# A four-part kernel on one core: router timing, weight splits, transposes and staging pools merged into one change

## The chip, the core and the metric

The kernel runs on one core of a Trainium2 chip. The core has five engines that run side by side and wait for each other through semaphores: TensorE for matmuls (PE in the profile; PEld are its weight loads), VectorE (DVE), ScalarE (ACT), GpSimd (POOL) and SyncE (SP). DMAs are issued from queues of SP, ACT and POOL. The metric is the device time of one execution in microseconds (us); lower is better. The text gives the median of several executions, and the profile shows one of them.

## The reference

The input x has 32 sequences of 128 tokens with 512 features, 4096 tokens in all. Four layers follow, the second and fourth with a residual around the pair they close:

```python
x = x + L0_ffn(L0_cond(x, cond))
x = x + L1_ffn(L1_cond(x, tokens, cond))

# L0_cond: two of eight experts per token, and one shared expert
shared = silu(x @ sw1.T) * (x @ sw3.T) @ sw2.T
s      = sigmoid(x @ router_w.T + cond @ router_t_w.T)   # the second term: one bias per sequence and expert
top2 of s + router_bias; gates from s; routed = sum of gate * (gelu(x @ rw1) @ rw2)
out    = (shared + routed) / 3
# L0_ffn: one of eight experts per sequence, chosen by its last token
logits = gelu(h[:, -1] @ Wp1 + bp1) @ Wp2 + bp2 ; sel = argmax(softmax(logits))
out    = h + 0.3 * ((gelu(h @ W1[sel] + b1[sel]) @ W2[sel] + b2[sel]) @ Wo + bo)
# L1_cond: one of 16 experts per token, given by a hash of the token, 256 slots each
xk, xr = mixes of x and the token before it
r      = sigmoid(xr @ w_recept.T) ; out = r * (relu(xk @ w_key) ** 2 @ w_value)
# L1_ffn: a scan over the 32 sequences as steps
f = sigmoid(x_t @ wf.T + c @ uf.T + bf); i, g likewise with wi, ui and wc, uc (g: tanh)
c = f * c + i * g
out = tanh(x @ wo.T + c_final @ uo.T + bo)
```

All data are float32.

## The kernel before, in words

Matmuls are made of split numbers. `split` (L61) writes a rounded copy, the high part, with ACT (L63) and the remainder, the low part, with DVE (L64). `mm3` (L76) then issues three matmuls for each block of 128 (L81): high by high, high by low, low by high. So every weight and every activation passes ACT and DVE once before PE may use it. `mm` (L54) is a plain matmul. A tile framework places the tiles in pools, adds the waits, and keeps the program's order on each engine except where its planner moves work; `tc.issue_after(ins)` orders what follows behind `ins` on the engine that `ins` runs on, and `behind` (L71) does it for both halves of a split.

The stages follow each other with little overlap:

- **A, 0 to about 310 us: the shared expert of token groups 0 to 3** (a group has 512 tokens, NG = 8). `shared` (L215) goes through eight weight columns a group (`KF`), each with `up`, `down` and the hooks `mid` and `hook2`. The weights come in pieces (`fetch_sw`, `split_sw`: raw tile swr, split swu and swd) through the raw pool of six buffers (L158). Group 0 also carries the router. `fetch_r` (L375) loads one 128-feature block of another group of x, `router` (L380) splits it and does the matmuls for rt with the router weights rwa and rwb, and zt is the copy of rt out of PSUM (L394). `mid0` (L592) spreads the 32 blocks over 16 half-steps by `cut` (L589), and calls `seq_bias` (L359), which sums the 512 features of cond times router_t_w over partitions by a matmul with ones into ps_tb. `choose`, `slots` and `invert` make the lists of tokens per expert. At the very start `fetch_x` (L203) loads group 0 on SP, and three copies of bias rows into the DRAM tensor bias_d (L726) stand on SP too.
- **Routed experts, about 310 to 558 us**: 71 blocks of 128 gathered tokens (xg, ptx, xb; `r_up`, `turn_h`, `r_down`), stored to o_d.
- **Shared expert of groups 4 to 7, 558 to 836 us**, with kept weights (kept_u), while `combine` (L747) adds shared and routed results, stores hid_d, and `policy` (L770) picks each sequence's expert. `hook2` (L939) calls, in the last group, `split_w` (L878) for the first three expert weights of the next stage, at the columns c = KF - AHEAD to KF - 1 with AHEAD = 3. `split_w(i)` splits piece i and then has `fetch_w(i + 3)` (L859) gather the next raw piece (rawB, 1 MB) by an indirect DMA on POOL into a pool of three buffers (wg, L711).
- **B, 836 to 1457 us: the per-sequence expert of L0_ffn and the mixes of L1_cond.** The loop over b (L1183 on) takes the sequences in an order sorted by expert, so that a weight is split anew only where the expert changes, four times. Iteration b does `up` (pu, then ue by ACT), `bend` (transposes pt, Gelu hf, split hb), `down` (po, then ps by ACT), and for the sequence before it `turn_r` (L1069): four transposes of ps into pr, then four times ACT with the bias (L1079) and DVE (L1080), which write the two halves of rT. Two sequences make a pair c. `close` (L1086) does the Wo matmuls of a pair (pb), adds the residual (x1, dx, xk) and, until the change, calls `mix_r` (L1134) for the other mix. In the odd iterations `send_k` (L1148: transposes ptB of xk, rows, a store to xk_d) and `send_v` (L1158: matmuls pv, r, a store to v_d) send the pair before. PSUM for all transposes of this stage is a pool of two buffers (ps_tB, L976); pt, pr and ptB take turns in it.
- **D, 1457 to 1834 us: the hashed experts** (`fetch_rows` gathers rowsD from xk_d by an indirect DMA; ptD transposes them; `use_piece` and its splits wD).
- **F, 1834 to about 2500 us: the scan.** `weight` (L1373) loads a 512x512 matrix in parts through a staging pool and splits it. `get_y` (L1406) gathers a block's y and loads r; `gate_y` (L1423) multiplies them, transposes (ptF) and splits into z. `from_x` and `from_c` (L1445, L1452) are the matmuls with z and with c. Until the change the staging pool is called stage and lives only for uf, wc, wi and wf (L1527 to L1540). After the last matmul a tail of output work follows up to the end.

Of the kernel before, what the change touches and what calls it, by code (L numbers as in the profile page):

```python
# [48 lines left out]
def tile_kernel(ctx: ExitStack, tc: tile.TileContext, a: dict, out: bass.AP):  # L49
# [106 lines left out]
    with ExitStack() as sa:  # L156
# [6 lines left out]
        def fetch(src, name):  # L163
            t = raw_p.tile([P, D], F32, tag="raw", name=name)
            nc.sync.dma_start(out=t, in_=src)
            return t

# [35 lines left out]
        def fetch_x(g):  # L203
            if g < NG:
                x_raw[g] = [fetch(a["x"][g][:, k, :], f"xraw_{g}_{k}") for k in range(KD)]
# [68 lines left out]
        with ExitStack() as s0:  # L274
# [31 lines left out]
            fetch_sw(1)  # L306
            ps_acc = s0.enter_context(tc.tile_pool(name="ps_acc0", bufs=4, space=PSUM, **kw))
# [51 lines left out]
            def seq_bias():  # L359

                ps = ps_r.tile([P, NB, E0], F32, tag="r", name="ps_tb")
                for k in range(KD):
# [7 lines left out]
                    mm(ps, ones, pr, k == 0, k == KD - 1)  # L370
# [218 lines left out]
            def cut(m):  # L589
                return min(NR, KD + (NR - KD) * (m - 1) // 15) if m > 0 else 0  # L590

            def mid0(n, w):  # L592

                if n < KF:
                    m = 2 * n + w
                    for i in range(cut(m), cut(m + 1)):
                        router(i)
                    for i in range(cut(m + 1), cut(m + 2)):
                        fetch_r(i)
                    if n + w == 1:  # L600
                        seq_bias()
# [124 lines left out]
        for kind, i in BIAS.items():  # L726
            nc.sync.dma_start(out=bias_d[:, bass.ts(i, KD)], in_=a[kind][:, KD * D :])
# [147 lines left out]
        def bias_of(kind, b, o):  # L875
            return bcol[b][:, BIAS[kind] * KD + o : BIAS[kind] * KD + o + 1]
# [21 lines left out]
        with ExitStack() as s2:  # L898
# [40 lines left out]
            def hook2(g, c):  # L939
                sums(g, c)  # L940
                if g == last:
# [22 lines left out]
    with ExitStack() as sb:  # L964
# [37 lines left out]
        def seq(p):  # L1002

            if p not in seqs:
                seqs[p] = nc.sync.value_load(seq_i[0:1, p : p + 1], min_val=0, max_val=PARTS[where(p)[0]] - 1)
            return seqs[p]

        def rows_of(t, p):

            return t[bass.ds((seq(p) + where(p)[0] * PARTS[0]) * P, P), :]  # L1010
# [58 lines left out]
        def turn_r(b):  # L1069
# [7 lines left out]
            for o in range(KD):  # L1077
                hi = rTs[c][:, 0, o, bass.ts(j, P)]
                done_a = nc.scalar.activation(hi, pt[:, o, :], AF.Identity, bias=bias_of("W2a", b, o))  # L1079
                done_v = nc.vector.scalar_tensor_tensor(  # L1080
                    rTs[c][:, 1, o, bass.ts(j, P)], pt[:, o, :], bias_of("W2a", b, o),
                    hi.bitcast(F32), ALU.add, ALU.subtract,
                )
            return done_a.ins, done_v.ins
# [63 lines left out]
        def send_k(b):  # L1148
# [5 lines left out]
            done = nc.scalar.copy(rows, pt.rearrange("p k q -> p (k q)"))  # L1154
            nc.sync.dma_start(out=rows_of(xk_d, b), in_=rows)
            return done.ins
# [21 lines left out]
        for b in range(-1, NB + 1):  # L1178
            c, j = divmod(b - 1, PB)
            if b + 1 < NB:  # L1180
# [28 lines left out]

            pair = b - 3 if b % 2 and 0 <= b - 3 < NB - 2 else None  # L1210
# [15 lines left out]
            if pair is not None and pair < NB - 6:  # L1226
                send_v(pair)
            if b + 1 < NB:
                bend(b + 1, "b")
            if pair is not None and pair < NB - 6:  # L1230
                send_v(pair + 1)
            if j == PB - 1 and 0 <= c < NB // PB:
                wo_done, k_done = close(c, b == NB)
                fetch_xh(c + 1)
                if c < NB // PB - 2:
                    mix_r(c, bp, "xr")
                elif c == NB // PB - 2:
                    mix_r(c, end_p, "xr")
# [3 lines left out]
        for b in range(NB - 2, NB):  # L1242
            rows_done = send_k(b)
# [11 lines left out]
    with ExitStack() as sd:  # L1255
# [97 lines left out]
        for p in range(NPC):  # L1353
# [14 lines left out]
            if p == NPC - 9:  # L1368
# [4 lines left out]
                def weight(name, pool, stage, bufs, tag="raw", parts=2, queue=nc.sync):  # L1373

                    pair = pool.tile([P, 2, KD * D], FR, tag=name, name=f"{name}_hl")
# [14 lines left out]
    with sf:  # L1390
        kw = dict(reuse_waits="tile")
        ZS = 2
        uf_p = sf.enter_context(tc.tile_pool(name="uf_p", bufs=1, side="right", **kw))
# [12 lines left out]
        def get_y(b):  # L1406

            y = yp.tile([P, D], F32, tag="y", name=f"y_{b}")
            nc.gpsimd.indirect_dma_start(  # L1409
# [5 lines left out]
            ys[b] = (y, r)  # L1415

        LEAD = 2
        for b in range(LEAD):
            get_y(b)
# [3 lines left out]
        def gate_y(b):  # L1423
# [11 lines left out]
            split(zs[g][:, 0, :, s], zs[g][:, 1, :, s], pt)  # L1435
# [9 lines left out]
        def from_x(t, ps, which, start, stop):  # L1445
            g, j = divmod(t, GB)
            for n in which:
                if start:
                    ps[n] = ps_g.tile([P, D], F32, tag="g", name=f"ps_{n}_{t}")
                mm3(ps[n], lambda h, k: zs[g][:, h, k, bass.ts(j, P)], lambda h, k: wx[n][:, h, k, :], KD, start, stop)  # L1450

        def from_c(t, n, ps, cT, start, stop):  # L1452
            if start:
                ps[n] = ps_g.tile([P, D], F32, tag="g", name=f"ps_{n}_{t}")
            mm3(ps[n], lambda h, k: cT[:, h, k, :], lambda h, k: uc[n][:, h, k, :], KD, start, stop)
# [16 lines left out]
        def unit(n, k0=0, k1=KD):  # L1472
# [15 lines left out]
            elif g >= NG - 1 - ZS:  # L1488
                zos[g, o] = zop.tile([P, GT], F32, name=f"zok_{g}_{o}")
# [237 lines left out]
```

## Time and profile before

| what | us |
|---|---|
| median of three runs | 2526.67 |
| the runs | 2529.47, 2526.67, 2520.85 |
| the profiled execution | 2522.89 |
| its span | 2521.2 |
| PE busy / idle in the span | 2455.6 / 65.6 |
| PE idle by stage: 0:310, 310:558, 558:836, 836:1457, 1457:1834, 1834:2500, 2500:2521 | 12.7, 2.2, 1.1, 19.5, 3.9, 5.0, 21.0 |
| DVE busy by the same stages | 237.5, 125.0, 177.1, 284.3, 262.4, 231.2, 14.1 |
| ACT busy by the same stages | 153.9, 97.3, 94.6, 316.4, 235.7, 158.1, 8.5 |
| mean granted TensorE clock of the span | 0.989 |

A busy share says how long an engine had an instruction in hand; the matmuls are pipelined, so a busy PE can still be slow, which the granted clock shows (1.00 is full speed). In the lists of waits a line names the engine and the instruction that stood still, what it stood for after the arrow, and then the time in all, how often, and the longest. In a list of stretches each engine's busy time stands before its number of instructions, and the granted clock, the DMA share and GB/s come last.

### The profile page before, as it was taken

The page shows a single profiled execution, that of the slowest core. Times are in us where ns is not written, and L with a number is a line of the kernel's source. Part 1 is how long each engine was busy: PE and PEld are TensorE (multiplying, and loading weights), DVE is VectorE, ACT ScalarE, POOL GpSimd, SP SyncE. Part 2 cuts the span into 40 slices and gives each one's busy share as a digit, 9 for nine tenths or more (in the row PEclk, how much of TensorE's full clock was granted, in tenths as well). Part 3 has the DMA queues.
Part 4 walks back from the last instruction along what each step waited for, and adds up shares of the span by engine and source line. Part 5 has one row for each costly group of instructions (what it writes and reads, how often), then busy time and mean ns, then how long its engine had stood idle before and what let it go on. Part 6 is the DMA issues. An engine that isn't in the chain of part 4 may idle for free. (4 is left out here: it accounts for less than half of the span.)

```text
span 2521.2 us, 37055 instructions
## 1 busy us (share of the span) xinstructions
PE 2455.6 (97%) x13044; PEld 2074.9 (82%) x13044; DVE 1331.5 (53%) x2341; ACT 1064.6 (42%) x1935; POOL 429.6 (17%) x460
## 2 busy tenths in 40 slices
PE   8999999999999899999999999999999999999996
PEld 5688899987888788888887889999978888888885
DVE  7797644556567444444454477667643323333336
ACT  4444533343223555455455466666532212222224
POOL 1000022222233333323223010000010000000003
PEclk9999999999999999999999999999999999999998
DMA  5545544457565333342342387776441111111027
GB/s 180 165 125 168 180 151 154 156 184 249 176 217 168 113 107 127 116 134 70 104 146 96 123 295 226 231 234 224 139 160 42 38 38 38 43 42 42 25 80 267
DMA packets 193117, 351.11 MB, mean 139 GB/s; under 512 B 37473, under 2 KB 72337, under 8 KB 189857
## 3 DMA queue, kind: packets, MB, share of 16 engines
q1 hardware_dynamic: 141504, 244.42, 29.6%
q0 software_dynamic: 36160, 74.90, 10.3%
q10 hardware_dynamic: 15264, 29.37, 3.2%
q8 instruction: 108, 1.77, 0.3%
q14 instruction: 81, 0.66, 0.1%
HBM read 373.94 MB, written 88.13 MB: 183 GB/s over the span
## 5 line engine op out<-in xcount | busy, mean ns | idle before, releaser
L64 DVE TENSOR_TENSOR wD<-rawD,wD 128x1024 fp32r<-128x1024 f32 x128 | 156.4, 1229 | 77.4 <-ACT wD L63 77.2
L81 PE MATMUL p<-xhl,swu 128*128 128x512 f32 x768 | 188.0, 396 | 5.5 <-ACT xhl L63 5.5
L81 PEld LDWEIGHTS phD<-xe,wD 128*128 128x128 f32 x1536 | 184.6, 189 | 1.2
L81 PE MATMUL phD<-xe,wD 128*128 128x256 f32 x1536 | 185.3, 281 | 0.0
L81 PE MATMUL p<-xhl,kept_u 128*128 128x512 f32 x768 | 184.3, 394 | 0.7 <-DVE kept_u L64 0.7
L81 PE MATMUL poD<-wD,hD 128*128 128x512 f32 x768 | 181.3, 392 | 0.0
L81 PEld LDWEIGHTS p<-xhl,swu 128*128 128x128 f32 x768 | 143.8, 189 | 36.0 <-ACT xhl L63 5.8
L81 PEld LDWEIGHTS p<-xhl,kept_u 128*128 128x128 f32 x768 | 141.8, 188 | 30.1 <-DVE kept_u L64 1.1
L81 PEld LDWEIGHTS poD<-wD,hD 128*128 128x128 f32 x768 | 142.0, 188 | 28.4
L63 ACT CAST wD<-rawD 128x1024 fp32r<-128x1024 f32 x128 | 133.1, 1046 | 53.4 <-PE poD L81 48.7
L278 POOL DMA_INDIRECT xg<-in_x_rows_dram,blk_t x71 | 67.6, 952 | 463.4 <-PE ptx L288 257.8
L1409 POOL DMA_INDIRECT y<-res_d,gat_i x32 | 33.3, 1040 | 573.9 <-DVE r L1428 495.2
L81 PE MATMUL pur<-r,xb 128*128 x852 | 118.2, 288 | 0.7 <-DVE xb L64 0.4
L81 PE MATMUL por<-r,hbr 128*128 x426 | 116.3, 407 | 1.4 <-ACT hbr L63 1.3
L64 DVE TENSOR_TENSOR xb<-ptx,xb 128x512 fp32r<-128x512 f32 x71 | 49.1, 692 | 115.3 <-ACT xb L63 115.3
L81 PEld LDWEIGHTS pur<-r,xb 128*128 128x128 f32 x852 | 105.2, 189 | 1.7 <-ACT xb L63 0.7
L81 PE MATMUL ps_f<-wf_hl,z 128*128 128x512 f32 x384 | 96.5, 399 | 0.0
L81 PE MATMUL poF<-z,wo_hl 128*128 128x512 f32 x384 | 96.4, 399 | 0.0
L81 PE MATMUL acc<-swd,as 128*128 128x512 f32 x384 | 96.0, 395 | 0.0
L81 PE MATMUL ps_c<-wc_hl,z 128*128 128x512 f32 x384 | 95.1, 395 | 0.7 <-ACT z L63 0.7
L81 PE MATMUL pb<-rT,Wo_hl 128*128 128x256 f32 x768 | 94.6, 281 | 0.0
L81 PE MATMUL pv<-w_recept_hl,xr 128*128 128x512 f32 x384 | 94.3, 395 | 0.0
(1014 smaller groups left out, 5038.3 us busy)
## 6 DMA issues: line engine op xcount, KB each, us to landing
rawD<-in_w_key_dram SPq DMA_DIRECT2D x64, 512.0 KB, 4.1
rawD<-in_w_value_dram SPq DMA_DIRECT2D x64, 512.0 KB, 3.8
swr<-in_sw_dram SPq DMA_DIRECT2D x120, 256.0 KB, 3.7
o_d<-obr SPq DMA_DIRECT2D x71, 256.0 KB, 2.4
xraw<-in_x_dram SPq DMA_DIRECT2D x32, 256.0 KB, 3.8
rraw<-in_rw_dram SPq DMA_DIRECT2D x32, 256.0 KB, 3.4
xc<-in_x_dram SPq DMA_DIRECT2D x32, 256.0 KB, 3.5
hid_d<-o ACTq DMA_DIRECT2D x32, 256.0 KB, 2.2
```

What stands on the lines that cost most here:

```text
L63: first = nc.scalar.copy(hi, src).ins
L64: done = nc.vector.tensor_tensor(lo, src, hi.bitcast(F32), ALU.subtract).ins
L81: done = nc.tensor.matmul(ps, lhsT=left(hl, k), rhs=right(hr, k), start=start and k + n == 0, stop=stop and 3 * k + n == last,)
L278: nc.gpsimd.indirect_dma_start(out=xg[i], out_offset=None, in_=a["x_rows"], in_offset=bass.IndirectOffsetOnAxis(ap=blk_t[:, i : i + 1], ax ...
L1409: nc.gpsimd.indirect_dma_start(out=y, out_offset=None, in_=res_d, in_offset=bass.IndirectOffsetOnAxis(ap=gat_i[:, b : b + 1], axis=0),)
```

## The change

It merges four edits to separate stages with some at the start:

- `fetch_x`: the pieces k = 0 and 2 of group 0 are issued by ACT, the others by SP.
- Router: `cut` starts at the fourth half-step instead of the second, router loads have six buffers of their own (xrr) and run two half-steps ahead. `seq_bias` adds the four products on DVE and uses one matmul group; it is called at the end of group 0.
- The bias rows are copied behind the last store of the routed experts.
- `split_w` for the first three pieces of stage B runs at c = 4, 5, 6.
- `turn_r`: one DVE add of the bias over the whole tile and one split. `mix_r` moves to the odd iteration after `close`; `send_v` moves to the even iterations, before `turn_r` and after `down`.
- The helpers `fetch`, `seq`, `rows_of`, `send_k`, `weight` and `bias_of` take a queue, a tile or a count as an argument; `get_y`, `gate_y`, `from_x` and `from_c` return their last instruction. `first_loads` is the last load of `fetch_sw(1)`.
- The last two `send_k` store from ACT's queue, with the row number read by ACT.
- Scan: one staging pool zop of four buffers for wc, uf, wi (SP) and wf (POOL), which later also holds the zok tiles; wo is staged after the second z, and the f matmuls of step 0 follow its c and i.

The diff without those helpers:

```diff
...
@@ -202,7 +204,10 @@
             if g < NG:
-                x_raw[g] = [fetch(a["x"][g][:, k, :], f"xraw_{g}_{k}") for k in range(KD)]
+                x_raw[g] = [
+                    fetch(a["x"][g][:, k, :], f"xraw_{g}_{k}", nc.scalar if g == 0 and k % 2 == 0 else nc.sync)
+                    for k in range(KD)
+                ]
...
@@ -358,7 +364,7 @@
-                ps = ps_r.tile([P, NB, E0], F32, tag="r", name="ps_tb")
+                sum_ = None
                 for k in range(KD):
@@ -367,7 +373,11 @@
                     )
-                    mm(ps, ones, pr, k == 0, k == KD - 1)
+                    if k > 0:
+                        nc.vector.tensor_tensor(pr, pr, sum_, ALU.add)
+                    sum_ = pr
+                ps = ps_r.tile([P, NB, E0], F32, tag="r", name="ps_tb")
+                mm(ps, ones, sum_, True, True)
                 nc.vector.tensor_copy(tbias, ps)
@@ -375,7 +385,9 @@
                 if 0 < g < NG:
-                    xrs[i] = fetch(a["x"][g][:, k, :], f"xr_{g}_{k}")
+                    xrs[i] = rt.tile([P, GT], F32, tag="xrr", bufs=6, name=f"xr_{g}_{k}")
+                    with tc.issue_after(first_loads):
+                        nc.sync.dma_start(out=xrs[i], in_=a["x"][g][:, k, :])
@@ -587,7 +599,7 @@
             def cut(m):
-                return min(NR, KD + (NR - KD) * (m - 1) // 15) if m > 0 else 0
+                return min(NR, KD + (NR - KD) * (m - 3) // 13) if m > 2 else 0
@@ -595,10 +607,8 @@
                         router(i)
-                    for i in range(cut(m + 1), cut(m + 2)):
+                    for i in range(cut(m + 2), cut(m + 3)):
                         fetch_r(i)
-                    if n + w == 1:
-                        seq_bias()
@@ -606,6 +616,8 @@
                     next(steps[0], None)
+                    if c == KF - 1:
+                        seq_bias()
                     return
@@ -723,8 +735,9 @@
-        for kind, i in BIAS.items():
-            nc.sync.dma_start(out=bias_d[:, bass.ts(i, KD)], in_=a[kind][:, KD * D :])
+        with tc.issue_after(stored):
+            for kind, i in BIAS.items():
+                nc.sync.dma_start(out=bias_d[:, bass.ts(i, KD)], in_=a[kind][:, KD * D :])
         os_, shs = {}, {}
...
@@ -943,9 +956,9 @@
                             fetch_w(n)
-                    if c >= KF - AHEAD:
+                    if 4 <= c < 4 + AHEAD:
                         with behind(act_split):
-                            split_w(c - KF + AHEAD)
+                            split_w(c - 4)
...
@@ -1074,14 +1089,13 @@
                 rTs[c] = rTp.tile([P, 2, KD, PB * P], FR, tag="rT", name=f"rT_{c}")
-            for o in range(KD):
-                hi = rTs[c][:, 0, o, bass.ts(j, P)]
-                done_a = nc.scalar.activation(hi, pt[:, o, :], AF.Identity, bias=bias_of("W2a", b, o))
-                done_v = nc.vector.scalar_tensor_tensor(
-                    rTs[c][:, 1, o, bass.ts(j, P)], pt[:, o, :], bias_of("W2a", b, o),
-                    hi.bitcast(F32), ALU.add, ALU.subtract,
-                )
-            return done_a.ins, done_v.ins
+
+            rT = ps.rearrange("p (k q) -> p k q", k=KD)
+            bias = bias_of("W2a", b, 0, KD).unsqueeze(2).to_broadcast([P, KD, P])
+            nc.vector.tensor_tensor(rT, pt, bias, ALU.add)
+            s = bass.ts(j, P)
+            split(rTs[c][:, 0, :, s], rTs[c][:, 1, :, s], rT)
+            return tuple(last_split)
...
@@ -1182,11 +1195,16 @@
                 fetch_hid(b + 3)
+            gated = b - 4 if b % 2 == 0 and 0 <= b - 4 < NB - 6 else None
+            if gated is not None:
+                send_v(gated)
             if 0 <= b - 1 < NB:
...
                 used()
+            if gated is not None:
+                send_v(gated + 1)
             if b == -1:
@@ -1206,6 +1224,10 @@
+
+            if j == 0 and 0 < c < NB // PB:
+                with behind(last_split) if b + 1 < NB else nullcontext():
+                    mix_r(c - 1, end_p if c == NB // PB - 1 else bp, "xr")
@@ -1223,24 +1245,16 @@
                 used()
-            if pair is not None and pair < NB - 6:
-                send_v(pair)
             if b + 1 < NB:
                 bend(b + 1, "b")
-            if pair is not None and pair < NB - 6:
-                send_v(pair + 1)
             if j == PB - 1 and 0 <= c < NB // PB:
...
                 fetch_xh(c + 1)
-                if c < NB // PB - 2:
-                    mix_r(c, bp, "xr")
-                elif c == NB // PB - 2:
-                    mix_r(c, end_p, "xr")
...
         for b in range(NB - 2, NB):
-            rows_done = send_k(b)
+            rows_done = send_k(b, nc.scalar)
         with tc.issue_after(k_done), tc.issue_after(rows_done):
...
@@ -1390,6 +1405,8 @@
+
+        zop = sf.enter_context(tc.tile_pool(name="zop", bufs=4, side="right", **kw))
         uf_p = sf.enter_context(tc.tile_pool(name="uf_p", bufs=1, side="right", **kw))
...
@@ -1486,7 +1505,9 @@
             elif g >= NG - 1 - ZS:
-                zos[g, o] = zop.tile([P, GT], F32, name=f"zok_{g}_{o}")
+                if o % 2 == 0:
+                    zok = zop.tile([P, 2, GT], F32, tag="raw", name=f"zok_{g}_{o}")
+                    zos[g, o], zos[g, o + 1] = zok[:, 0, :], zok[:, 1, :]
                 nc.scalar.copy(zos[g, o], po)
@@ -1524,21 +1545,23 @@
         ps, wx = {}, {}
-        with tc.tile_pool(name="stage", bufs=4, side="right", **kw) as stage:
-            uc["f"] = weight("uf", uf_p, stage, 4)
-            for b in range(LEAD):
-                nc.scalar.activation(ys[b][1], ys[b][1], AF.Sigmoid)
-            for n in "cif":
-                from_c(0, n, ps, cT, True, False)
-            wx["c"] = weight("wc", wx_p, stage, 4, queue=nc.scalar)
-            with tc.issue_after(first_part["wc"]):
-                gate_y(0)
-                gate_y(1)
-            for b in range(LEAD):
-                get_y(b + LEAD)
-            for n in "if":
-                wx[n] = weight("w" + n, wx_p, stage, 4, queue=nc.scalar)
-        zop = sf.enter_context(tc.tile_pool(name="zop", bufs=1, **kw))
+
+
+        wx_hl = {n: wx_p.tile([P, 2, KD * D], FR, tag="w" + n, name=f"w{n}_hl") for n in "ifc"}
+        wx["c"] = weight("wc", wx_p, zop, 4, pair=wx_hl["c"])
+        uc["f"] = weight("uf", uf_p, zop, 4)
+        wx["i"] = weight("wi", wx_p, zop, 4, pair=wx_hl["i"])
+        for b in range(LEAD):
+            nc.scalar.activation(ys[b][1], ys[b][1], AF.Sigmoid)
+        for n in "cif":
+            from_c(0, n, ps, cT, True, False)
+        gate_y(0)
+        z_done = gate_y(1)
+
+        with tc.issue_after(first_got):
+            wx["f"] = weight("wf", wx_p, zop, 4, pair=wx_hl["f"], queue=nc.gpsimd)
+        for b in range(LEAD):
+            get_y(b + LEAD)
         bias = {n: load_row("b" + n, D, keep_p) for n in "cif"}
@@ -1546,13 +1569,16 @@
             if t == 0:
-                from_x(0, ps, "cif", False, True)
-                wo1 = weight("wo", keep_p, yp, 2, "zo", KD)
+                done = from_x(0, ps, "ci", False, True)
+                with tc.issue_after(done):
+                    from_x(0, ps, "f", False, True)
+                with tc.issue_after(z_done):
+                    wo1 = weight("wo", keep_p, yp, 2, "zo", KD)
                 for n in "cif":
...
                 for n in "cif":
-                    from_c(t, n, ps, cT, False, True)
+                    late = from_c(t, n, ps, cT, False, True)
                     gate(t, n, ps, v, bias)
@@ -1589,8 +1615,9 @@
                     split(uo1[:, 0, k], uo1[:, 1, k], raw)
-                load_part(first_p, "c0", "x", 3, 0)
-                load_part(first_p, "cT0", "x", 3, 1, 2)
+                with tc.issue_after(late):
+                    load_part(first_p, "c0", "x", 3, 0)
+                    load_part(first_p, "cT0", "x", 3, 1, 2)
                 load_part(yp, "zo", "x", 3, 3)
...
             if t == NB - 2:
```

More of the change, by code (lines that the diff above doesn't have):

```diff
@@ L161, in tile_kernel, with fetch @@
         xgp = sxg.enter_context(tc.tile_pool(name="xgp", bufs=3, **kw))
-        def fetch(src, name):
+        def fetch(src, name, queue=nc.sync):
             t = raw_p.tile([P, D], F32, tag="raw", name=name)
-            nc.sync.dma_start(out=t, in_=src)
+            last_load[:] = [queue.dma_start(out=t, in_=src).ins]
             return t
+        last_load = []
         NSW = KF * NG
@@ L306, in tile_kernel @@
             fetch_sw(1)
+            first_loads = last_load[0]
             ps_acc = s0.enter_context(tc.tile_pool(name="ps_acc0", bufs=4, space=PSUM, **kw))
@@ L873, in fetch_w, with bias_of @@
                     )
-        def bias_of(kind, b, o):
-            return bcol[b][:, BIAS[kind] * KD + o : BIAS[kind] * KD + o + 1]
+        def bias_of(kind, b, o, n=1):
+            return bcol[b][:, BIAS[kind] * KD + o : BIAS[kind] * KD + o + n]
         def split_w(i):
@@ L1000, in tile_kernel, with seq, rows_of @@
         seqs, end_p = {}, None
[L1002 to L1010, printed above, removed]
+        def seq(p, queue=nc.sync):
+            if (p, queue) not in seqs:
+                seqs[p, queue] = queue.value_load(
+                    seq_i[0:1, p : p + 1], min_val=0, max_val=PARTS[where(p)[0]] - 1
+                )
+            return seqs[p, queue]
+        def rows_of(t, p, queue=nc.sync):
+            return t[bass.ds((seq(p, queue) + where(p)[0] * PARTS[0]) * P, P), :]
         xs = {}
@@ L1146, in mix_r, with send_k @@
             split(xrs[c][:, 0], xrs[c][:, 1], dx)
-        def send_k(b):
+        def send_k(b, queue=nc.sync):
             c, j = divmod(b, PB)
@@ L1153, in send_k @@
             rows = rp.tile([P, D], F32, tag="rows", bufs=2, name=f"rows_{b}")
-            done = nc.scalar.copy(rows, pt.rearrange("p k q -> p (k q)"))
-            nc.sync.dma_start(out=rows_of(xk_d, b), in_=rows)
-            return done.ins
+            nc.scalar.copy(rows, pt.rearrange("p k q -> p (k q)"))
+            return queue.dma_start(out=rows_of(xk_d, b, queue), in_=rows).ins
         def send_v(b):
@@ L1371, in tile_kernel, with weight @@
                 uc, first_part = {}, {}
-                def weight(name, pool, stage, bufs, tag="raw", parts=2, queue=nc.sync):
-                    pair = pool.tile([P, 2, KD * D], FR, tag=name, name=f"{name}_hl")
+                def weight(name, pool, stage, bufs, tag="raw", parts=2, queue=nc.sync, pair=None):
+                    if pair is None:
+                        pair = pool.tile([P, 2, KD * D], FR, tag=name, name=f"{name}_hl")
                     flat = a[name].rearrange("p k n -> p (k n)")
@@ L1408, in get_y @@
             y = yp.tile([P, D], F32, tag="y", name=f"y_{b}")
-            nc.gpsimd.indirect_dma_start(
+            got = nc.gpsimd.indirect_dma_start(
                 out=y, out_offset=None, in_=res_d,
@@ L1415, in get_y @@
             ys[b] = (y, r)
+            return got.ins
         LEAD = 2
         for b in range(LEAD):
-            get_y(b)
+            first_got = get_y(b)
         zp = sf.enter_context(tc.tile_pool(name="zp", bufs=2, **kw))
@@ L1434, in gate_y @@
             s = bass.ts(j, P)
-            split(zs[g][:, 0, :, s], zs[g][:, 1, :, s], pt)
+            return split(zs[g][:, 0, :, s], zs[g][:, 1, :, s], pt)
         def turn(c, t):
@@ L1449, in from_x @@
                     ps[n] = ps_g.tile([P, D], F32, tag="g", name=f"ps_{n}_{t}")
-                mm3(ps[n], lambda h, k: zs[g][:, h, k, bass.ts(j, P)], lambda h, k: wx[n][:, h, k, :], KD, start, stop)
+                done = mm3(ps[n], lambda h, k: zs[g][:, h, k, bass.ts(j, P)], lambda h, k: wx[n][:, h, k, :], KD, start, stop)
+            return done
         def from_c(t, n, ps, cT, start, stop):
@@ L1454, in from_c @@
                 ps[n] = ps_g.tile([P, D], F32, tag="g", name=f"ps_{n}_{t}")
-            mm3(ps[n], lambda h, k: cT[:, h, k, :], lambda h, k: uc[n][:, h, k, :], KD, start, stop)
+            return mm3(ps[n], lambda h, k: cT[:, h, k, :], lambda h, k: uc[n][:, h, k, :], KD, start, stop)
         def gate(t, n, ps, v, bias):
```

## The prediction

> **What bounds the kernel now.** I read the busy times first, then what the tensor engine (PE) waits for, then the clock around the longest waits, then single rows. The page's first line:
>
> ```profile
> PE 2455.6 (97%) x13044; PEld 2074.9 (82%) x13044; DVE 1331.5 (53%) x2341; ACT 1064.6 (42%) x1935; POOL 429.6 (17%) x460
> ```
>
> PE is the bound: of 2521.2 us it is idle for 65.6, of which 21.6 are the tail after the last matmul and 44 lie between matmuls. A matmul of 128x512 starts every 0.227 us (12 take 2.72), and the change touches almost none of them. So it can win holes, the slow clock behind holes, and few matmuls. The waits of PE (total us, times, longest) name the holes:
>
> ```profile
> PE pt_0a L1050 <- ACT ue_0a L1043: 7.0, 1, 7.0
> PE p L81 <- ACT xhl L63: 5.5, 1, 5.5
> PE ptD L1304 <- DMA rowsD<-xk_d,slot_t: 3.9, 3, 1.7
> PE rt L55 <- DVE rwa L356: 3.0, 1, 3.0
> PE ptF L1433 <- DVE z L64: 2.9, 1, 2.9
> PE pt_6a L1050 <- ACT o L756: 2.6, 1, 2.6
> PE ptB L1152 <- ACT hf_26a L1053: 2.5, 1, 2.5
> PE pt_15a L1050 <- DVEq L891: 2.1, 1, 2.1
> PE ptB L1152 <- ACT hf_16a L1053: 2.0, 1, 2.0
> PE ps_tb L55 <- ACT zt L394: 1.9, 1, 1.9
> ```
>
> Ten rows hold 33 of the 44 us, and all but the second lie in stages that the diff touches. Below them come nine waits of ptB for an hf of 0.2 to 0.5 us, 3 together. Stretches (PE, PEld, DVE, ACT, POOL busy, then the granted clock):
>
> ```profile
> 0.00:50.00 50.00, 39.61 (x155) 28.07 (x156) 32.40 (x77) 23.95 (x40) 8.95 (x28) 0.97 0.58 177
> 835.00:855.00 20.00, 13.04 (x52) 10.39 (x51) 7.12 (x11) 9.53 (x17) 7.21 (x7) 0.74 0.79 276
> 1834.00:1869.00 35.00, 30.65 (x129) 23.93 (x128) 20.20 (x26) 18.50 (x25) 10.43 (x9) 0.90 0.69 227
> ```
>
> A clock of 0.74 over 20 us is 5.2 us of clock missing. By the same product: 1.5 in 0 to 50, 1.8 at 930 to 950 (0.91), 1.6 at 1105 to 1145 (0.96), 1.5 at 1315 to 1330 (0.90), 3.4 at 1455 to 1470 (0.77), 3.5 at 1834 to 1869. Everywhere else in the middle it is full. So holes of about 2 us and more cost again behind them.
>
> **The skill.** "TensorE: Matmul & The Clock Gate", What's actually happening: half the clock after an idle window of about 3.4 us, full again after a busy one, with a window that runs on its own. The trace agrees in size (one piece is worth 1.5 to 1.8, half of 3.4) but not in the threshold: holes of 1.9 to 2.6 us brought it on too. "DMA: Bandwidth & Descriptors", Issuing engines are not separate DMA queues: another issuing engine saves only issue time. The trace agrees: the first weight and the x pieces land some 1.1 us apart per 256 KB, so part 1 is priced at nothing. "ScalarE: Activation LUTs", What ACT_TABLE_LOAD costs: 1.28 us for a load; the trace has 1.28 at 12.88, and part 7 meets one.
>
> **The change, part by part** (against the profiled execution of 2522.9 us; it is 3.8 below the median of 2526.7, inside the runs' spread of 8.6).
>
> 1. *Two of the first x pieces issued by ACT, bias rows away from the start.* First matmul still at 5.5: 0 (-0.5 to +1).
>
> 2. *Router from the fourth sub-step on with its own six buffers; one matmul group for the biases, at the end of group 0.* The first router matmul waits 3.0 us for rwa, which the DVE makes at 17.75 behind setup work; four matmuls later nothing waits. The bias sum's hole is 1.9. Its matmuls:
>
> ```profile
> L55 PE MATMUL ps_tb<-pr,ones x16: 379/380/696, 28.7 to 34.4; 128*128 128x256 f32 x16
> ```
>
> Eight of them pass in 2.49 us, about half of it at the slow clock, so 0.25 each at full clock; a quarter remains, 12 x 0.25 = 3.0 less. Clock 1.5. Two waits for zt near 67 and 97 (1.0 and 1.1) move with the router; I count half, 1.0. Added: three DVE adds of 0.42. Sum 3.0+1.9+3.0+1.5+1.0 = 10.4, with a little of the mode switching gone 11 (4 to 13). The cover is the DVE: it is 83.4 of the first 110 us busy, and the router's same work is pressed from 15 into 13 sub-steps. On SP the weight pieces stand behind router loads, each waiting for one of six buffers until its split.
>
> 3. *Bias rows sent after the routed store.* Three SP issues of about 0.6 us stand ahead of swr_34; that piece was split at 565 to 568 and wanted at about 572, so it had 2 to 5 us in hand: +0.5 (0 to +3).
>
> 4. *The first three weight splits of stage B one column earlier (c = 4, 5, 6).* The stall at that stage's start:
>
> ```profile
> 845.38 1.04 ACT L63 CAST wB_W2b<-rawB 128x1024 fp32r<-128x1024 f32 x1 [7.39 <-DMA rawB<-in_W2b_dram,idxw]
> ...
> 846.54 0.59 ACT L1043 COPY ue_0a<-pu_0a 128x512 f32<-128x512 f32 x1
> ...
> 847.18 1.11 PE L1050 MATMUL pt_0a<-ident,ue_0a 128*128 128x128 f32 x4 [6.96 <-ACT ue_0a L1043]
> ```
>
> ue_0a stands on ACT behind the cast of W2b, whose gather was issued at 835.7 and took 9.7. The gather waits for the buffer that the split of W2a frees; one column (about 8 us) earlier it is issued at 827.5 and lands at 837, before ue_0a is wanted at 840.2 (where the hole begins). The hole of 7.0 goes, and of the 5.2 of clock the part in which matmuls ran (842.3 to 852.6 at half, the hole until 847.2: 5.4/2 = 2.7). Sum 9.7; 9 taken (5 to 10.5).
>
> 5. *Stage B.* turn_r's four ACT activations (0.37) and four DVE operations (0.35), each waiting for the other, become one DVE add (128x512 from PSUM, 0.69 as such rows take), one cast (0.62) and one subtract (0.69). DVE work is the same (1.40 and 1.38), ACT falls by 0.86 a sequence. The old form's waits:
>
> ```profile
> L1080 DVE SCALAR_TENSOR_TENSOR rT<-pr,b,rT x128: 339/351/355, 867.7 to 1438.0; 128x128 fp32r<-128x128 f32 x128
> ...
>   ACT rT L1079: 56.8, 56
> ```
>
> mix_r leaves close for the following odd step, behind the weight split; send_v goes to even steps, so ptB's transposes directly follow those of pt_a and no longer wait for Gelu (hf) to free a PSUM buffer. Gone: the four holes at expert changes 2.6+2.1+2.0+2.5 = 9.2, of which ptB keeps 2.6 (in two of them it now waits 1.3 for the add); the small waits, 3; clock 3.5 of 4.9; one switch between transposes and matmuls a pair, 0.2 by the rows' spacing, 15 times, 3. That is 16 if no new wait comes; I take two thirds, 11 (2 to 14).
>
> 6. *The last two key rows on ACT's queue.* rows_31's store waits for rows_30's landing, as before, and ACT now stands behind it for 2.75 us; r_28 and the last mix cast follow. The gathers of stage D come about 1.7 earlier: of the holes 3.9 and the clock 3.4, 2 are won (4 won to 2 lost).
>
> 7. *Start of the scan.* One pool of four staging buffers, order wc, uf, wi on SP, wf on POOL, wo after the second z. Before, PE waited 0.7 and 2.9 and 0.6 here. Now ACT must cast wc, uf and wi, load a table and take the two sigmoids before the first z; wi's pieces wait for the DVE to split wc (1837 to 1838), r behind them on SP lands 4 to 6 us later (SP's row of before: 5.44 for two issues). So ptF stands at 1847 to 1848, PE's last ps_f ends at 1842.4: one hole of about 5 instead of 4.2 in three, with the same clock behind: +1 (-3 to +6).
>
> 8. The scan's steady part and the tail keep their order on every engine: 0.
>
> Sum: 0-11+0.5-9-11-2+1 = -31.5. From the profile 2491.4, from the median 2495.2; **2494**.
>
> **Rivals.** *Half is won (2510).* Group 0 becomes DVE-bound (85% where the router is pressed together) or the weights come late behind router loads, part 2 gives 2 instead of 11; or B's holes merely change their owner, part 5 gives 3 and the start of the scan costs 4: -31.5+9 or +11 = -22 to -20 for one, -12 for both. For it: the wait for rwa names a DVE that is behind, and clock windows are all or nothing. Against: 25% of the DVE is free there.
>
> *The stage-B pair is now tied to the DVE (slower, 2553).* ptB needs turn_r's PSUM buffer, which only one DVE add frees; where this add stands behind a weight split (1.23 each, two a piece) PE waits in all 16 pairs. From about 2 us a pair on the clock falls too, 1.7: 3.7 x 16 = 59 on 2494. It decides from 2.4 us a pair without clock loss (39/16), from about 2 with it. Against: DVE was busy 25.4 of 60 us in steady B (870 to 930), and the add is its first work after pr; only expert changes come near.
>
> *The edits cancel (2526).* Clock windows move rather than vanish, scan start at +6, bias rows +3, ACT behind its own store +2. Needs three ends at once.
>
> *It doesn't do what it says.* The order that the scheduler gives after the change shows the moves: router after three sub-steps, ptB behind pt_a, four bias instructions. Excluded.
>
> **How the numbers follow.** Chances: all or most won 0.62, half 0.25, nothing 0.06, slower by a pair's wait or by the scan's start 0.07. About 0.3% (7.6 us) is what a measurement of this kernel can tell from no change, so faster is 0.87. The main case's own range is 2483 to 2506. For 8 in 10 the half case comes in: 2480 (ends of parts 2, 4, 5 and 6 together, -43) to 2515.
>
> **What would show it.** The waits of rt for rwa, ps_tb for zt and pt_0a for ue_0a absent; PEclk 1.0 in 0 to 50 after the first microseconds and near the start of stage B; ps_tb four instructions; ptB's waits for hf gone, at most two for DVE rT of 1 to 2 us; ptD's wait under 2.5; one ptF hole near 5. PE busy about 2440. The forecast is wrong if p waits for weight pieces in group 0, if ptB waits for rT in most pairs, or if the ptF hole passes 8.

## The result and the profile after

The changed kernel takes 2504.98 us (median of four runs, 2502.66 to 2510.3) against 2524.09 for the kernel before (the three runs above and one more of 2521.5): a ratio of 0.9926, with a 95% interval from 0.9904 to 0.9947. It is faster by 19 us where 31.5 were forecast, and inside the stated range. The profiled execution of the changed kernel is its slowest of the four, 2510.3 with a span of 2508.6, so the two profiles differ by 12.6 and not by 19.

The first line of the page and the waits of PE after the change (total us, times, longest):

```profile
PE 2446.4 (98%) x13030; PEld 2071.8 (83%) x13030; DVE 1332.5 (53%) x2275; ACT 1038.9 (41%) x1839; POOL 414.1 (17%) x462
```

```profile
PE po L81 <- DVE hb_0a L64: 7.1, 1, 7.1
PE p L81 <- ACT xhl L63: 6.3, 1, 6.3
PE acc L81 <- ACT as L63: 6.0, 1, 6.0
PE acc L81 <- DVE as L64: 2.6, 1, 2.6
PE phD L81 <- DVE hf L1337: 2.3, 1, 2.3
PE ptF L1451 <- DVE r L1446: 2.2, 1, 2.2
PE rt L55 <- DVE rwa L362: 2.1, 1, 2.1
```

PE is still idle for 62.2 us of the span (2508.6 less 2446.4), where it was idle for 65.6. The waits of ptB for hf, of pt_0a and pt_15a and of ps_tb are gone, and pt_6a waits 0.6 where it waited 2.6. New are two long ones, acc for as (8.6 us in two pieces) and po for hb_0a (7.1), a wait of 2.3 of phD for hf, and a few of under 2 us that are not shown here.

The stretches around them (PE, PEld, DVE, ACT, POOL busy, then the granted clock, DMA share and GB/s):

```profile
0.00:50.00 50.00, 41.61 (x172) 30.25 (x173) 39.18 (x106) 27.63 (x46) 8.77 (x28) 1.00 0.68 223
550.00:580.00 30.00, 20.68 (x75) 15.72 (x74) 16.70 (x29) 11.62 (x21) 8.00 (x11) 0.83 0.76 227
845.00:865.00 20.00, 12.87 (x51) 10.21 (x51) 3.78 (x6) 7.56 (x19) 4.99 (x5) 0.74 0.58 190
930.00:970.00 40.00, 38.96 (x216) 32.97 (x215) 24.57 (x37) 23.95 (x44) 13.27 (x14) 1.00 0.57 186
1824.00:1859.00 35.00, 32.11 (x135) 25.59 (x134) 19.25 (x25) 15.78 (x23) 9.09 (x11) 0.90 0.55 181
```

The slow clock left the first 50 us and the expert change at 930 to 970. It came to 550 to 580. At the start of stage B and of the scan it stayed.

Where the time went is easiest to see by stage. The landmarks are the first or last starts of groups of matmuls, and the stages are: A up to the first pur, R to the first p with kept_u, S to the last acc with kept_d, B0 to the first pb, B1 to the first ptD, D to the first ps_c with uc, F to the end of the span. All durations are differences of such starts in one profiled execution of each kernel. R and D are nearly untouched by any of the kernels of this text and show how far one profile may be trusted: over all fourteen, R lies between 248.8 and 252.1 and D between 375.2 and 379.9.

| kernel | A | R | S | B0 | B1 | D | F |
|---|---|---|---|---|---|---|---|
| before | 307.6 | 249.4 | 278.8 | 52.7 | 569.2 | 376.5 | 687.0 |
| after | 297.6 | 251.9 | 291.6 | 53.1 | 551.9 | 376.8 | 685.7 |
| after less before | -10.0 | +2.5 | +12.8 | +0.4 | -17.3 | +0.3 | -1.3 |

Stage A won what was forecast and stage B more. Stage S lost 12.8 where 0.5 had been allowed, and the start of stage B (B0) won nothing where 9 had been expected.

### The profile page after: what moved, and what is told of

Same layout as the page of the kernel before. It is cut to its first block, busy times and chain, and to the rows that moved or that the text cites. A ratio compares the mean times of both kernels' runs of the same rounds, so it can differ in the third digit from the quotient of the medians.

```text
span 2508.6 us, 36845 instructions
## 1 busy us (share of the span) xinstructions
PE 2446.4 (98%) x13030; PEld 2071.8 (83%) x13030; DVE 1332.5 (53%) x2275; ACT 1038.9 (41%) x1839; POOL 414.1 (17%) x462
## 4 chain that ended last, share of the span: by engine, by line
PE 49%; DVE 2%; DMA 1%; ACT 0%; issue 0%; POOL 0%; POOLq 0%; SPq 0%; DVEq 0%; ACTq 0%
PE phD L81 7%; PE ps_c L81 7%; PE ps_f L81 7%; PE ps_i L81 7%; PE poD L81 7%; PE poF L81 3%; PE po L81 3%; PE pb L81 2%; PE pv L81 2%; PE ptF L1451 1%; PE ptC L1458 1%; PE ptD L1318 0%; PE ptB L1166 0%; DMA rawD<-in_w_value_dram 0%; PE pr L1089 0%
## 5 line engine op out<-in xcount | busy, mean ns | idle before, releaser
L81 PE MATMUL acc<-kept_d,as 128*128 128x512 f32 x384 | 95.1, 398 | 8.6 <-ACT as L63 6.0
L747 POOL DMA_INDIRECT o<-o_d,s_i x64 | 63.6, 993 | 185.7 <-PE pth L767 99.2
```

Source lines behind the costliest of these rows:

```text
L81: done = nc.tensor.matmul(ps, lhsT=left(hl, k), rhs=right(hr, k), start=start and k + n == 0, stop=stop and 3 * k + n == last,)
L747: nc.gpsimd.indirect_dma_start(out=o[n], out_offset=None, in_=o_d, in_offset=bass.IndirectOffsetOnAxis(ap=idx[:, b : b + 1], axis=0),)
```

## The experiments

Each run was timed beside runs of the kernel before, to which its ratio is. Their median was 2522.4 to 2527.0 from one set to the next, so kernels of different sets are better compared by their ratios than by their times. The sets are the runs on the two holes and on the early splits; those on the start, on the bias rows, on all of stage B and the mended kernel; and the other four.

### The two new holes, one at a time

**Bias rows back at the start.** The edit on the changed kernel:

```diff
-        with tc.issue_after(stored):
-            for kind, i in BIAS.items():
-                nc.sync.dma_start(out=bias_d[...], in_=a[kind][:, KD * D :])
+        for kind, i in BIAS.items():
+            nc.sync.dma_start(out=bias_d[...], in_=a[kind][:, KD * D :])
```

> The changed kernel with one edit undone: the three bias rows are copied at the program's start again, as before. Theory: the holes of 6.0 and 2.6 us at 567 and 571 (acc for as) and the slow clock after them, 9.6 us in all, come from these copies, which hold SP for 5.7 us and the DMA engines longer, so that swr_34 lands at 564.9. Then no wait of acc is over 1 us, the clock is full from 550 to 580, and the time falls by 8 to 10 to about 2495. Rival: the weight pieces would be late there anyway, since stage A now leaves them another place in the queues; then the holes stay and the time stays at about 2505.

Measured: 2504.16 us, ratio 0.9925 (0.9911 to 0.9939), the same as the changed kernel. Yet S fell from 291.6 to 279.9, so the theory about the hole was right. The gain was given back in stage A, which rose from 297.6 to 305.7. (The two profiles differ by 8.4 us where the medians differ by 0.8: this kernel's profiled execution is its fastest, the changed kernel's is its slowest. The sum of all stages is not to be trusted to that size; these two stages come out the same in other kernels, as the table further below shows.) There PE has a new wait, and the clock of the first 50 us, full in the changed kernel, is 0.93, which is 3.5 us of clock:

```profile
PE p L81 <- ACT swu L63: 3.4, 1, 3.4
0.00:50.00 50.00, 37.74 (x141) 26.66 (x142) 32.65 (x81) 22.37 (x37) 8.82 (x28) 0.93 0.61 198
```

The wait is for a weight piece that comes late. The three copies are now issued one after the other (2.7, 3.4 and 5.7 us), not at 3.6, 17.2 and 17.8 as before. Stretches of this kernel:

```profile
6.00:8.00 2.00, 1.12 (x2) 0.61 (x3) 1.67 (x3) 1.88 (x4) 0.83 (x3) 1.00 1.13 317
8.00:10.00 2.00, 2.00 (x6) 1.52 (x6) 1.57 (x4) 1.24 (x2) 2.00 (x9) 1.00 0.56 36
10.00:12.00 2.00, 2.00 (x9) 1.62 (x8) 0.58 (x1) 0.00 (x0) 1.10 (x3) 1.00 0.06 2
```

For about 6 us, from 8 to 14, the DMA engines move 2 to 36 GB/s, although four weight pieces are issued from 8.7 on; they had moved 317 just before. The same trough stands in the changed kernel at 553, directly behind the copies' new place. SP's queue and the stretch there, and then what SP's queue (q1) and POOL's (q0) carried from 553 to 561: packets, MB and the share of the DMA engines' time. The last line is SP's queue in the kernel before from 560 to 568, at about the same place in its stage S:

```profile
552.43 4.13 SPq L740 DMA_DIRECT2D bias_d<-in_W2a_dram  x1
556.66 1.59 SPq L165 DMA_DIRECT2D swr<-in_sw_dram  x1
```

```profile
553.00:556.00 3.00, 3.00 (x15) 2.49 (x14) 1.75 (x5) 0.77 (x2) 1.00 (x1) 1.00 0.43 19
```

```profile
q0 software_dynamic: 180, 0.29, 22.6%
q1 hardware_dynamic: 2750, 0.07, 19.6%
q1 hardware_dynamic: 1595, 1.92, 78.9%
```

The third copy holds the queue for 4.1 us, and swr_34 is issued at 556.66 and lands at 564.87. In those 8 us SP's queue carries little but the copies' small rows, while the engines are busy for 42% of the time: they are not full, and the piece waits all the same. The two things that make it late, the held issue and the small rows ahead of it in the same queue, were not tried apart. ACT waits for it, and the work for as follows behind it on ACT and DVE (its subtraction, the product sg, the cast of as), so acc waits 6.0. The second piece of the hole, 2.6, is DVE waiting for shc, loaded by the same queue behind the copies; the subtraction for as stands next:

```profile
564.87 0.62 ACT L63 CAST kept_u<-swr 128x512 fp32r<-128x512 f32 x1 [10.64 <-DMA swr<-in_sw_dram]
566.85 0.62 ACT L63 CAST as<-sg 128x512 fp32r<-128x512 f32 x1 [1.36 <-DVE sg L238]
569.97 0.75 DVE L763 SCALAR_TENSOR_TENSOR o<-o,g,shc 128x512 f32<-128x512 f32 x1 [2.03 <-DMA shc<-sh_d]
570.64 0.68 DVE L64 TENSOR_TENSOR as<-sg,as 128x512 fp32r<-128x512 f32 x1
```

A copy is 1024 rows of four floats, 16 KB in all. The Trainium skill, "DMA: Bandwidth & Descriptors", Specifications, says that a transfer needs at least 512 bytes a piece for line rate, and that smaller ones are read, modified and written. The runs agree in direction, 19 GB/s in that stretch; they don't show the mechanism, nor why the rows pass so slowly while the engines have time.

**The first combine of stage B later.** In the changed kernel:

```diff
-            if 0 <= late < GB and step == 2:
+            if 0 < late < GB and step == 2:
                 combine(NB - GB + late, ps_t)
...
                 bend(b + 1, "a")
+            if late == 0 and step == 2:
+                with behind(last_split):
+                    combine(NB - GB, ps_t)
```

> The changed kernel with the first combine of stage B (sequence 28) ordered behind the split of hb_6a, so that its two DVE operations, which wait for the copy shc out of DRAM, no longer stand ahead of the subtraction for hb_0a. Theory: the 7.1 us that PE waits at 858 for hb_0a, and the slow clock behind, are this load alone; both go, stage B starts 9 to 10 us earlier and the time falls to about 2495. Rival: something else of the crowded DMA there (hid rows, Wo, the third or fourth weight) comes next and takes at least half of it; then 2500 or more.

Measured: 2501.17 us, ratio 0.9909 (0.9894 to 0.9925). B0 fell from 53.1 to 43.0, all of the 10 expected, and no wait of PE is left in it. Yet the time is only 4 us below the changed kernel's. B1 rose by 3.9, to 555.8, because the combine now came in the middle of an expert change, where its operation on DVE is late and PE's transposes for it wait 3.6 us:

```profile
PE pth L767 <- DVE o L764: 3.6, 1, 3.6
```

The hole that the combine had caused is seen in the timeline of DVE in the changed kernel:

```profile
855.90 0.75 DVE L763 SCALAR_TENSOR_TENSOR o<-o,g,shc 128x512 f32<-128x512 f32 x1 [10.52 <-DMA shc<-sh_d]
856.86 0.75 DVE L764 SCALAR_TENSOR_TENSOR o<-o,g,o 128x512 f32<-128x512 f32 x1 [0.21 <-DVEq L904]
857.53 0.69 DVE L64 TENSOR_TENSOR hb_0a<-hf_0a,hb_0a 128x512 fp32r<-128x512 f32 x1
```

DVE stands 10.5 us on an operation of the shared-expert sum, whose input makes a round trip through DRAM (shc, stored and loaded again; this load was issued at 846.0), and hb_0a, which PE wants, is next in line.

**Both at once.**

> Both at once, bias rows at the start and the first combine of stage B later. Theory: the two holes are independent, so the gains add: 18 to 20 below the changed kernel, about 2486, a ratio to before of about 0.985. Rival: they share a cause (the DMA engines' load or the position of the clock's window), and the sum is less than 14.

Measured: 2497.75 us, ratio 0.9897 (0.9882 to 0.9913), 7 below the changed kernel and not 18 to 20. The sum is as small as the rival said, but not for its reason, a common cause: by the stages, A 305.1, S 281.5, B0 43.1 and B1 555.4, each cure wins about what it won alone, 10 us each, and each brings its own cost along, 7.5 in A and 3.5 in B1.

### Was the hole of stage B hidden before?

The kernel before with the first three weight splits one column earlier (c = 4, 5, 6) and nothing else:

> The kernel before with only the first three weight splits of stage B one column earlier (c = 4, 5, 6). My forecast for this part alone was 9 us. Theory now: the load of shc for the first combine ended at the same time as the gather of W2b, at about 851, and so the hole of 7.0 only changes its owner, from pt_0a (ACT) to po (DVE, hb_0a); the time stays within 3 us of before. Rival: the load was made late only by the other edits; then the hole is under 2 us and the time is 8 to 10 below before.

Measured: 2524.34 us, ratio 1.0005 (0.9996 to 1.0014). B0 is 51.5 where it was 52.7. PE's wait of 7.0 for ue_0a is gone, and a wait of 6.8 for hb_0a stands in its place. The theory holds: two chains ended within a few us of each other before, and taking away one shows the other. The timeline of DVE in the kernel before had it:

```profile
851.39 0.81 DVE L750 SCALAR_TENSOR_TENSOR o<-o,g,shc 128x512 f32<-128x512 f32 x1 [2.06 <-DMA shc<-sh_d]
...
852.91 0.69 DVE L64 TENSOR_TENSOR hb_0a<-hf_0a,hb_0a 128x512 fp32r<-128x512 f32 x1
```

Even with the gather's delay ahead of it, DVE waited 2 us more for shc.

### Which edit won stage A

**The edits to the start and the router alone**, on the kernel before (x pieces on ACT, router later with its own buffers, one bias sum at the end of the group):

> The kernel before with the edits to the start and the router alone (two x pieces on ACT's queue, router from the fourth half-step with its own buffers, one bias sum at the end of group 0); the bias rows stay at the start. My forecast for these edits was 11 us. Theory A, as forecast: PE's holes for rwa and zt and twelve matmuls go, 9 to 12 us less, about 2512. Theory B: of the 11 us most came from the bias rows leaving the start, since three copies of 1024 small rows starve the weight loads; then 2 to 5 less, 2518 to 2521, and p or acc waits for a weight piece near 18.

Measured: 2524.91 us, ratio 0.9999 (0.9987 to 1.001). A is 305.5, 2.1 less than before (other kernels with the old start go down to 306.2), and PE waits 3.8 us for a weight piece at 18, as theory B said. Here too the three copies come one after the other (2.7, 3.4, 5.5), so this kernel has the worse form of the copies.

**The bias rows alone moved behind the last store**, on the kernel before:

> The kernel before with only the bias rows moved behind the last store of the routed experts. My forecast was half a microsecond more. Theory B: the start gains 4 to 8 and the stretch from 550 to 600 loses 8 to 10, so the sum is 0 to 4 above before. Theory A: the start gains nothing and the whole is 8 to 10 slower, 2531 to 2533.

Measured: 2532.26 us, ratio 1.0022 (1.0013 to 1.0031), which is 3 to 8 us slower and lies between the two theories. A is 304.8, 2.8 less; S is 290.4, 11.6 more. So the loss in S is the copies' alone, and it doesn't need the other edits. The gain in A is no sum: 2.1 for the router edits and 2.8 for the copies, but 10.0 with both. With the copies gone the router edits are worth 7.2 (304.8 to 297.6). Part of this may be that the router edits alone bunch the copies; the router edits with the copies spread as before were not run.

### What won stage B

**All edits of stage B and of its last stores alone**, on the kernel before:

> The kernel before with the edits of stage B and of its last stores alone (turn_r, mix_r, send_v, send_k on ACT's queue). Forecast 11 for stage B and 2 for the stores. Theory from the two traces: 17 to 18 in all between 900 and 1475, so about 2505. Rival: the gain needs the earlier start of stage B's weights or the scan's new order; then 11 or less, 2512 or more.

Measured: 2507.75 us, ratio 0.992 (0.9899 to 0.994). B1 is 551.6. That is all of the changed kernel's gain, as the theory said; the rest of the change cancels.

**turn_r alone**:

```diff
-            for o in range(KD):
-                hi = rTs[c][:, 0, o, bass.ts(j, P)]
-                done_a = nc.scalar.activation(hi, pt[:, o, :], AF.Identity, bias=...)
-                done_v = nc.vector.scalar_tensor_tensor(rTs[c][:, 1, o, ...], pt[:, o, :], ..., hi, ...)
+            nc.vector.tensor_tensor(rT, pt, bias, ALU.add)
+            split(rTs[c][:, 0, :, s], rTs[c][:, 1, :, s], rT)
```

> The kernel before with turn_r alone in its new form (one DVE add, one split); mix_r and send_v stay. Together with them and the last stores the stage gave 17 between 900 and 1425. Theory O: the order is what counts, ptB behind pt_a and not behind hf; then turn_r alone gives at most 4, the holes of 2 to 2.6 us for hf_16a and hf_26a stay, about 2522. Theory T: the old form's ping-pong kept ACT late and thereby hf; then turn_r alone gives 8 to 14 and those holes fall under 1 us.

Measured: 2514.3 us, ratio 0.9969 (0.9955 to 0.9983), B1 561.8, 7.4 less than before. The wait for hf_16a fell to 0.5, but in the place of hf_26a stands one of 2.1 that names DVE's queue.

**The moves of mix_r and send_v alone** (with the last stores on ACT's queue):

> The kernel before with the moves of mix_r and send_v (and the last stores on ACT's queue) alone; turn_r keeps its four ACT and four DVE operations. Theory O: 12 to 17 less, about 2511, with no wait of ptB for an hf. Theory T: under 6, since ptB's buffer is now freed only by the ping-pong, and PE waits there for DVE rT in many pairs.

Measured: 2520.93 us, ratio 0.9987 (0.9978 to 0.9996), B1 566.2, 3.0 less. The waits of PE in stage B of this kernel:

```profile
PE ptB L1154 <- DVE rT L1082: 6.8, 7, 3.7
PE pt_6a L1052 <- DVE rT L1082: 2.3, 1, 2.3
```

Theory O missed both runs. Theory T had this one right (under 6, with PE waiting for rT) and was just too high for the one before (8 to 14 against 7.4). It doesn't say what the two give together, though. The moves free ptB from Gelu and hand it to turn_r, since ptB now takes the PSUM buffer that turn_r frees; with four operations in turn on two engines turn_r frees it late. One DVE add frees it in 0.69. Alone the two are worth 7.4 and 3.0, together 17.6 (569.2 to 551.6).

### The scan's start

The changed kernel with the scan's staging as before:

> The changed kernel with the scan's start as before (staging pool, order uf, wc, wi, wf on two queues). My forecast for the change there was 1 us lost. From the two traces: 8.4 us above the plain matmul times before and 7.2 after, so this is 0 to 2 slower than the changed kernel. Rival: the new start loses up to 4 elsewhere, in the last matmuls of stage D; then this is faster than the changed kernel.

Measured: 2510.33 us, ratio 0.995 (0.9933 to 0.9968); the interval overlaps the changed kernel's. F is 688.3 against 685.7. One profile would not settle 2.6 us, but all eight kernels with the old start have an F of 687.0 to 688.6 and all six with the new one 683.9 to 685.9. The new order is some 2 us better.

### A version that keeps the gains

The changed kernel, with the copies among the routed experts and all combines of stage B two sequences later:

```diff
+                if i in (10, 25, 40):
+                    kind = ("W1a", "W1b", "W2a")[(i - 10) // 15]
+                    with tc.issue_after(stored):
+                        nc.sync.dma_start(out=bias_d[...], in_=a[kind][:, KD * D :])
...
-            late, step = divmod(b - 3, 3)
+            late, step = divmod(b - 5, 3)
```

and the first combine behind a split, as above.

> The changed kernel with the three bias rows copied one at a time behind the routed experts' stores 9, 24 and 39 (310 to 500 us), and the combines of stage B two sequences later, the first of them behind the split of hb_8a. Theory: a single copy of small rows among the routed blocks is hidden, since PE works there from weights in place and the loads run three blocks ahead; both the hole at 570 and that at 858 go and none comes at 935, so about 22 below the changed kernel, 2482 to 2486. Rival: each copy stalls the gathers of xg for 2 to 4 us and PE waits there; then 2490 or more.

Measured: 2489.31 us (2488.16 to 2490.31), ratio 0.985 (0.9833 to 0.9867), 15.7 below the changed kernel by the medians and 19 by the ratios. The stages: A 297.3, R 251.4, S 279.3, B0 43.0, B1 553.9, D 376.8, F 685.9. Each gain is kept except 2 us in B1, where a later combine has PE wait 1.6 for pv. The expected 2482 to 2486 was missed by 3, in a set in which the kernel before took 2527.0. A copy among the routed blocks shows no hole: in the stretches with the copies of 336.3 and 387.9 PE stays busy, as in this one.

```profile
389.00:392.00 3.00, 3.00 (x23) 2.74 (x22) 1.74 (x3) 0.90 (x3) 0.95 (x1) 1.00 0.65 113
```

**The three copies in one place**, behind one routed store:

> The mended kernel with the three bias copies one behind the other at store 24 instead of 15 blocks apart. Theory: place decides; the gathers run three blocks (10 us) ahead and a bunch starves the loads for about 6, so it stays within 2 us of the mended kernel. Rival: bunching itself costs, since the third copy holds the queue until the first two are through, PE waits for xb near the copies and 3 to 8 us are lost.

Measured: 2492.7 us (2489.16 to 2498.35), ratio 0.9887 (0.9868 to 0.9906). The profiled span is 2487.4, that of the mended kernel 2487.6, and R 252.0 against 251.4; PE waits once near the copies, 1.0 us for hbr. By the medians it is 3.4 slower, by the ratios, whose sets differ, about 9, and by the profile nothing. The profiled execution is the fastest of four that reach from 2489.16 to 2498.35. Whether bunching costs stays open; that the place matters, and not only the number of copies, is clear beside the 11.6 of stage S.

Put together, the stages of all fourteen kernels fall into groups, and their ranges don't overlap. This is firmer than any single pair of profiles:

| stage and its form | kernels | us |
|---|---|---|
| A as before | 5 | 306.2 to 308.7 |
| A, copies moved, router as before | 1 | 304.8 |
| A, router edits, copies one after the other at the start | 3 | 305.1 to 305.7 |
| A, router edits, no copies there | 5 | 297.3 to 300.0 |
| S with the copies right ahead of it | 4 | 290.4 to 293.0 |
| S without | 10 | 278.1 to 281.6 |
| B0, first combine as before | 10 | 51.0 to 53.1 |
| B0, first combine later | 4 | 43.0 to 43.1 |

## Why the prediction was right or wrong

The direction, the range and the kind of mechanism (holes and the clock behind them) were right. The size was six tenths of the forecast by the medians and four tenths by the two profiles, and that the sum came into the range is in part luck: parts 3 and 4 came out 12.3 and 9.4 worse than forecast, and part 5 came out 6.3 better. By the stages of the two profiles:

- **Parts 1 and 2, 0 and -11: measured -10.0, with half of the reason.** Part 1 gave the bias rows nothing ("First matmul still at 5.5: 0") and part 2 gave all to the router. Yet putting the rows back takes away 8.1 of the 10.0 (305.7), and the router edits without their leaving are worth 2.1. In the kernel before, the stretch that follows the second and third copy was there to read: it has a trough of 7 GB/s at 20 to 22 us, and ACT then waits for an xr. The copy zt, for which the bias sum waited 1.9, stands right behind:

```profile
20.00:22.00 2.00, 2.00 (x11) 1.09 (x9) 2.00 (x7) 1.22 (x4) 0.00 (x0) 1.00 0.23 7
27.43 0.62 ACT L63 CAST xrhl<-xr 128x512 fp32r<-128x512 f32 x1 [4.35 <-DMA xr<-in_x_dram]
27.96 0.57 ACT L394 COPY zt<-rt 16x512 f32<-16x512 f32 x1
```

So that hole, priced under the router, was the copies' too, and with the copies alone moved it is gone. The wait for rwa, forecast to vanish, is still 2.1: PE comes to it at 16.9 where it came at 15.0, but DVE makes rwa at 18.7 where it made it at 17.8.
- **Part 3, +0.5: measured +12.8 in S, 11.6 with this edit alone.** The failed step is "Three SP issues of about 0.6 us". That is what a copy takes with an empty queue ahead. The third took 4.13, and the copies' 3072 small rows, which no term of the sum counted, filled SP's queue ahead of the weight pieces and of shc. The upper bound of 3 came from the same wrong unit, so it couldn't hold either.
- **Part 4, -9: measured +0.4.** The ACT part happened as worked out: the gather was issued at 832.9, landed by 838.7, and the wait for ue_0a went. The failed step is "The hole of 7.0 goes". I asked what ended the hole and not what would have ended it next. The load of shc, issued 839.8 and waited for until 851.4, was on DVE's timeline ahead of hb_0a.
- **Part 5, -11: measured -17.3.** The step "That is 16 if no new wait comes; I take two thirds" was the wrong one; the full sum was nearly right. ptB and pt_6a wait 0.5 and 0.6 for the add where 2.6 had been left. The experiments add what the sum didn't say: turn_r and the moves are worth less apart (10.4) than together.
- **Part 6, -2: measured nothing that shows.** It was not run alone. ptD's wait fell from 3.9 to 1.9, and phD got one of 2.3 for hf behind it; D is 376.8 after 376.5.
- **Part 7, +1: measured -1.3.** The mis-sized term is the time at which wi's staging comes free: it took uf's buffers and was issued at 1816.45, so r was issued at 1818.0 and not behind a split at 1837. The holes were 2.2 and 0.7, not 5, with 3.5 us of clock lost behind, as forecast.

Of the rivals, "half is won" had about the right time and the wrong place: neither DVE nor the router loads starved group 0. The slower one, ptB tied to turn_r, is real where turn_r keeps its old form; the seven waits of the kernel with the moves alone are that wait. One DVE add is short enough.

## What to carry to other kernels

Before a hole is counted as won, read the other engines in the same stretch for the chain that ends next; here a wait that ended within a few us of it took its place. Price a DMA by its rows and by what stands behind it in the same queue, not by its bytes or its issue time, and put small-row copies where nothing is loaded just in time. Two edits on one buffer's life can each be worth little and together much, so cost the buffer's whole cycle and not each edit.

## What the runs showed of the hardware

Three DRAM copies of 1024 rows of 16 bytes, 48 KB in all, kept the DMA engines at 2 to 36 GB/s for about 6 us at the start, and the third copy's issue took 2.3 to 4.3 us of SP's queue over the eight kernels that bunch them, where a single one took 0.5 to 0.7. The engines had time to spare meanwhile (busy shares of 0.06 to 0.56), and the pieces that waited stood in the same queue as the rows. I had not expected 48 KB to cost 8 to 12 us of a kernel that is 98% matmul. The clock is as little predictable as in the kernel before: a hole of 1.6 us for pv at 1081 in the mended kernel brought no slow stretch, one of 1.4 for xb at 500, with another of 0.3 close behind, did.
